# A layernorm inside a local transformer: statistics by token rows on VectorE, applied by GpSimd, in place of sums by matmul

## The chip, the cores and the metric

The kernel runs on one core of a Trainium2 chip. A core has five engines that run their own instruction streams and meet at semaphores: TensorE (PE; its weight loads are listed apart as PEld), VectorE (DVE), ScalarE (ACT), GpSimd (POOL) and SyncE (SP), which here only issues DMA transfers. The metric is the device time of one execution in microseconds. The kernel before takes 4091.11 us, the median of three runs between 4088.63 and 4092.11.

## The reference

Two transformer blocks with adaptive layernorm over 16 sequences of 256 tokens by 128 channels, all in fp32. The first block has a linear attention, and in the place of its feed-forward part a whole local transformer of six layers. That inner transformer is where the change lies:

```python
for i in range(DEPTH):                       # 6 layers
    x = attn_layer(shift_tokens(x), ...) + x # 16 heads of 64, windows of 32 tokens
    x = ffn_layer(shift_tokens(x), ...) + x

def ffn_layer(x, g, bln, W1, b1, W2, b2):
    mu = x.mean(-1, keepdims=True)
    var = ((x - mu) ** 2).mean(-1, keepdims=True)
    xn = (x - mu) / jnp.sqrt(var + 1e-05) * g + bln
    hg = xn @ W1 + b1
    a, gate = jnp.split(hg, 2, -1)
    return a * jax.nn.gelu(gate, approximate=False) @ W2 + b2
```

The mean and the variance go over the 128 channels of a token. The local attention normalises each q and k head, rotates it, takes scores over the own window and the one before, a softmax, and a weighted sum. The second block is an attention with relative position bias and a plain feed-forward part.

## The kernel before

The work is cut into 8 units of two sequences, 512 tokens each. Activations are held with the channels on the partitions and the tokens along the free axis: a tile is 128x512. The state of the inner transformer stays in SBUF for all six layers, one tile `zs[u]` for each unit, with a margin of 32 columns for the window before and one column for the shift of tokens.

The kernel has three stages: the first block's attention (to about 265 us), the local transformer (to about 3525 us) and the second block. The local transformer is one software pipeline written as a loop over `n` (L1065). A turn of the loop starts one pair of head groups (two of the eight pairs of heads) of one unit, so a unit takes four turns, a layer 32, and the six layers 192; the work that belongs to earlier turns is done in the same turn, with lags of 1 to 10. Around the change, a turn does this in order:

- GpSimd scales two k by their inverse norms (`scaled`, L802); these come from DRAM by the transfer kn.
- TensorE merges the weighted values into the output (`merging`, L942); after the unit's fourth merge the attention's result is added to the state (L955).
- In odd turns TensorE turns the inverse norms rk upright (`norms_rows`, L781), VectorE copies them (L783), and SyncE stores them (rkh, L785), from where kn is read (`widened`, L793).
- GpSimd rotates q and k of the turn before (`rotate`, four instructions at L721), using `got`, a copy of VectorE's `sent` with swapped partitions that SyncE makes by DMA (L715, L716).
- TensorE flips the probabilities (L906, copied by VectorE at L911); GpSimd divides the next ones (L898).
- In even turns the sums of squares (L729), copied by ScalarE (L738); then the weighted sums (L921), copied out by ScalarE (L936) and VectorE (L934); then the scores (L858), on VectorE their maxima (L870, L872).
- In even turns `norms_inverse`: TensorE turns the sums (L747), VectorE makes a first guess (L749, L758), and GpSimd does three Newton steps (L765 to L773), which end in rk (L772) and rq.
- The next two projections of q and k (L705): ScalarE squares them (L708) between the exponentials (L880), and VectorE writes `sent` (L710) and r (L713) for each.

The feed-forward part of a unit is a generator, `ffn(u, i)`. Its pieces are put into the turns by `go_on(behind)`, which is called four times in a turn: after the flips (L1098), after the weighted sums (L1111), after `norms_inverse` (L1127), and after the first of the two projection pairs (L1134). A `yield` ends a piece. The first piece of a unit comes at L1127 in the turn of its last merge, the second at L1134 of that turn, the third at L1098 of the next; four yields are one turn. So the pieces are: the mean (L968) and its subtraction (L970); the square (L973); the variance, the power and a copy of the inverse deviations over 128 columns (L977, L985, L987, L989); one turn later the turning of these and the scaling (L994, L995, L996); then at one turn's distance the gates (L1004, L1006), the other half (L1014, L1018) and the last matmul with the addition to the state (L1027, L957). Units follow one another every four turns, so each period of four turns has one call's first piece and the later pieces of the call before.

The order on TensorE, VectorE, ScalarE and GpSimd is the order in which the program is written (`manual_schedule`, L130 to L135 and L1062). SyncE's queue is not in that list, and the trace shows its transfers in another order than that of the program.

Matmul results go through four PSUM banks that are handed round (`bank()`, L58, with `psum(es, 4, 3)` at L601): the fifth allocation waits until the first is read out. In a feed-forward tile pool with one buffer each lie `fx` and `fs`, which this function uses.

Of the kernel before, what the change touches and what calls it, by code (L numbers as in the profile page):

```python
# [14 lines left out]
ALU = mybir.AluOpType  # L15
# [29 lines left out]
def adaln_kernel(  # L45
# [12 lines left out]
    def bank():  # L58
        return stage["ps"].tile([128, 512], F32, tag="mm", name="mm")

    def two(ap):
        return ap.rearrange("p (s t) -> p s t", s=2)
# [537 lines left out]
    with ExitStack() as es:  # L600
# [362 lines left out]
        def ffn(u, i):  # L963


            src = zs[u][:, :, PAD : PAD + L]
            pm = bank()
            nc.tensor.matmul(pm, mean128, src, start=True, stop=True)  # L968
            xn = ftile("fx")
            nc.vector.tensor_tensor(two(xn), src, two(pm), ALU.subtract)  # L970
            yield
            sq = ftile("fs")
            nc.scalar.activation(sq, xn, AF.Square)  # L973
            yield
            pv = bank()
            for t in range(4):
                nc.tensor.matmul(  # L977
                    pv[:, t : t + 1],
                    sq[:, t * 128 : (t + 1) * 128],
                    mean128[:, 0:1],  # L980
                    start=True,
                    stop=True,
                )
            ve = small("ve", (128, 4))
            nc.vector.tensor_scalar(ve, pv[:, 0:4], 1e-5, None, ALU.add)  # L985
            rs = small("rs", (128, 4))
            nc.gpsimd.tensor_tensor(rs, ve, half[:, 0:4], ALU.pow)  # L987
            ex = ftile("fs", (128, 4, 128))
            nc.gpsimd.tensor_copy(ex, rs.unsqueeze(2).to_broadcast([128, 4, 128]))  # L989
            for _ in range(4):  # L990
                yield
            rb = bank()
            for t in range(4):
                nc.tensor.transpose(rb[:, t * 128 : (t + 1) * 128], ex[:, t], ident)  # L994
            nc.vector.tensor_tensor(xn, xn, rb, ALU.mult)  # L995
            nc.vector.tensor_scalar(xn, xn, bcol(i, "g"), bcol(i, "b"), ALU.mult, ALU.add)  # L996
            for _ in range(4):
                yield
            w1, w2 = wffs[i]
            gates = []  # L1000
            for c, n in enumerate(FFC):
                pg = bank()
                c0 = FFH + c * 128
                nc.tensor.matmul(pg[0:n, :], w1[:, c0 : c0 + n], xn, start=True, stop=True)  # L1004
                gt = ftile("fg", bufs=3)
                nc.scalar.activation(gt[0:n, :], pg[0:n, :], AF.Gelu, bias=bcol(i, f"g{c}", n))  # L1006
# [14 lines left out]
            yield  # L1021
            yield
            yield
            yield
            py = bank()
            for c, n in enumerate(FFC):
                nc.tensor.matmul(  # L1027
                    py, w2[0:n, c, :], gates[c][0:n, :], start=(c == 0), stop=(c == 2)
                )
            add_to_state(u, py, bcol(i, "b2"))  # L1030
# [589 lines left out]
```

## Time and profile before

| | |
|---|---|
| median of three runs | 4091.11 us (4088.63 to 4092.11) |
| profiled execution, span from first to last instruction | 4089.6 us |
| local transformer, of this | about 265 to 3525 us |
| TensorE's granted clock, mean | 0.980; 1.00 between 1000 and 3440 us |
| time from one unit's mean (L968, L970) to the next unit's | 63.5 to 70 us |

The page gives no other time of the profiled execution than its span; what lies around it can only be read from the runs, whose median is 1.5 us above.

In the views below a line of the chain of waits has a start, a length and then engine, tile and line of the code; it follows the work that ended last back through what released it. A line of a timeline has start, length, engine, line, operation, output and inputs with their shapes, and how many were put together; in brackets stands the time for which the engine was idle before, with what ended it. "mm" is any of the four rotating PSUM banks, "fx" and "fs" the tiles of the feed-forward part, "rs" the inverse deviations, "z" the state. TensorE is listed with two passes for a matmul in fp32, so a matmul counts as two instructions; a turning (transpose) counts as one.

### The profile page before, as it was taken

How to read it: one execution, taken by the hardware profiler on the slowest of the kernel's cores; microseconds unless marked ns; L12 is line 12 of the kernel's file. 1: busy time of each engine (PE TensorE's matmuls, PEld its weight loads, DVE VectorE, ACT ScalarE, POOL GpSimd, SP SyncE). 2: the span in 40 equal slices, each digit the busy share in tenths (PEclk: the TensorE clock that was granted, in tenths of full speed). 3: DMA queues.
4: the chain of work that ended last, by engine and by line, in shares of the span. 5: the costliest groups of instructions: out<-in, count | busy, mean ns of one | idle time of the engine just before them, and what ended most of it. 6: DMA issues, size and time to landing. Idle time of an engine off the chain costs nothing.

```text
span 4089.6 us, 117058 instructions
## 1 busy us (share of the span) xinstructions
PE 3824.8 (94%) x44534; PEld 2533.5 (62%) x44534; DVE 2944.4 (72%) x6006; ACT 2797.5 (68%) x9683; POOL 2653.6 (65%) x3374
## 2 busy tenths in 40 slices
PE   7877899999999999999999999999999999799998
PEld 4534666666666666666666666666666666455554
DVE  6756777777777777777777777777777775476664
ACT  4536777777777777677777777776777776366665
POOL 6437777767776777677776777777777665255453
PEclk9878999999999999999999999999999999899999
DMA  1334454445545445454554444454545443200000
GB/s 42 42 83 118 121 126 115 123 118 128 126 124 127 117 122 125 117 127 113 128 131 121 121 123 116 123 130 120 127 107 131 115 118 79 63 1 6 9 6 9
DMA packets 316617, 408.82 MB, mean 100 GB/s; under 512 B 48745, under 2 KB 212632, under 8 KB 316056
## 3 DMA queue, kind: packets, MB, share of 16 engines
q1 hardware_dynamic: 316056, 401.33, 39.6%
q8 instruction: 353, 5.78, 0.6%
q14 instruction: 208, 1.70, 0.1%
HBM read 178.26 MB, written 21.56 MB: 49 GB/s over the span
## 4 chain that ended last, share of the span: by engine, by line
PE 53%; DVE 16%; ACT 16%; issue 6%; POOL 5%; DMA 2%; SPq 1%; ACTq 0%; DVEq 0%; POOLq 0%
PE mm L921 8%; ACT pr L880 7%; PE y L942 6%; PE mm L705 6%; PE sim L858 6%; DVE sent L710 3%; PE mm L729 3%; PE mm L1027 3%; ACT sq L708 2%; PE mm L1014 2%; PE mm L1398 2%; DVE mx L870 2%; PE mm L906 2%; PE sim L1325 2%; DVE k L713 2%
## 5 line engine op out<-in xcount | busy, mean ns | idle before, releaser
L880 ACT ACTIVATE pr<-sim,nb,rq 128x64 f32<-128x64 f32 x3072 | 1229.2, 453 | 366.9 <-DVE nb L872 307.5
L880 ACT ACTIVATION_READ_ACCUMULATOR pr<-sim,nb,rq 128x1 f32 x3072 | 783.1, 255 | 0.0
L942 PEld LDWEIGHTS y<-zx,wvo 128*128 128x128 f32 x6144 | 715.8, 192 | 93.0 <-issue 88.3
L802 POOL TENSOR_TENSOR k<-k,kn 128x512 f32<-128x512 f32 x384 | 483.7, 1274 | 435.9 <-DMA kn<-rkh 434.4
L705 PE MATMUL mm<-z,wqk 128*128 128x512 f32 x1536 | 710.3, 604 | 13.4 <-DMA wqk<-in_L_ffn_Wqkv_dram 7.9
L942 PE MATMUL y<-zx,wvo 128*128 128x128 f32 x6144 | 717.9, 275 | 2.2 <-ACT zx L936 1.8
L721 POOL TENSOR_TENSOR q<-q,got 128x512 f32<-128x512 f32 x384 | 488.5, 1272 | 300.4 <-DMA got<-sent 173.2
L710 DVE SCALAR_TENSOR_TENSOR sent<-mm,vec,rope 128x512 f32<-128x512 f32 x768 | 571.0, 743 | 117.4 <-ACT sq L708 109.9
L934 DVE COPY zx<-mm 128x512 f32<-128x512 f32 x384 | 255.3, 674 | 375.0 <-PE mm L921 374.5
L708 ACT ACTIVATE sq<-mm 128x512 f32<-128x512 f32 x768 | 475.6, 619 | 30.9 <-PE mm L705 29.5
L721 POOL TENSOR_TENSOR k<-k,got 128x512 f32<-128x512 f32 x384 | 496.4, 1293 | 0.0
L705 PEld LDWEIGHTS mm<-z,wqk 128*128 128x128 f32 x1536 | 281.9, 192 | 328.5 <-issue 252.5
L921 PE MATMUL mm<-prT,xw 64*128 64x256 f32 x3072 | 452.5, 401 | 11.6 <-ACT n L738 6.4
L921 PEld LDWEIGHTS mm<-prT,xw 64*128 64x128 f32 x3072 | 326.7, 188 | 179.9 <-DVE rsum L893 38.6
L898 POOL TENSOR_TENSOR pr<-pr,rsum 128x512 f32<-128x512 f32 x384 | 392.3, 1043 | 14.0 <-PE mm L1004 7.4
L936 ACT COPY zx<-mm 128x512 f32<-128x512 f32 x384 | 227.0, 596 | 248.9 <-PE mm L921 248.4
L870 DVE TENSOR_REDUCE mx<-sim 128x8 f32<-128x512 f32 x384 | 263.1, 685 | 138.7 <-PE sim L858 137.9
L1368 POOL TENSOR_TENSOR pr<-pr,rsum 128x256 f32<-128x256 f32 (+1 forms) x256 | 205.1, 832 | 242.2 <-DVE rsum L1366 218.2
L858 PEld LDWEIGHTS sim<-k,q 64*32 64x32 f32 x24576 | 264.3, 106 | 80.9 <-issue 56.4
L858 PE MATMUL sim<-k,q 64*32 64x64 f32 x24576 | 299.5, 227 | 11.8 <-POOL k L802 6.5
L1354 ACT ACTIVATE pr<-lg,nm 128x128 f32<-128x128 f32 (+1 forms) x512 | 226.3, 443 | 117.3 <-DVE nm L1343 109.4
L713 DVE SCALAR_TENSOR_TENSOR q<-mm,vec,rope 128x512 f32<-128x512 f32 x384 | 284.5, 741 | 0.0
(253 smaller groups left out, 6244.7 us busy)
## 6 DMA issues: line engine op xcount, KB each, us to landing
got<-sent SPq DMA_DIRECT2D x1536, 128.0 KB
kn<-rkh SPq DMA_DIRECT2D x768, 128.0 KB
xw<-rows SPq DMA_DIRECT2D x384, 128.0 KB
rows<-xt SPq DMA_DIRECT2D x96, 128.0 KB
wqk<-in_L_ffn_Wqkv_dram SPq DMA_DIRECT2D x48, 128.0 KB
bhome<-brow SPq DMA_DIRECT2D x1, 3072.0 KB
wv<-in_L_ffn_Wqkv_dram SPq DMA_DIRECT2D x12, 256.0 KB
wo<-in_L_ffn_Wo_dram SPq DMA_DIRECT2D x12, 256.0 KB
```

Source lines behind the costliest of these rows:

```text
L705: nc.tensor.matmul(pp, wqk[:, j, :], xs, start=True, stop=True)
L708: nc.scalar.activation(sq, pp, AF.Square)
L710: nc.vector.scalar_tensor_tensor(two(sent[:, j, :]), two(pp), scale, tab[1], ALU.mult, ALU.mult)
L713: nc.vector.scalar_tensor_tensor(r, two(pp), scale, tab[0], ALU.mult, ALU.mult)
L721: nc.gpsimd.tensor_tensor(r, r, two(got[:, j, :]), ALU.add)
L802: nc.gpsimd.tensor_tensor(k, k, two(kn), ALU.mult)
L858: nc.tensor.matmul(sims[par][32 * c : 32 * c + 32, c0 : c0 + 64], q[r, s, t0 : t0 + 32], k[r, s, t0 : t0 + 64], start=False, stop=True, sk ...
L870: nc.vector.tensor_reduce(mx, sim.rearrange("p (b k) -> p b k", b=8), AX.X, ALU.max)
L880: nc.scalar.activation(pr[:, x, st, par, :], sims[par][:, b * 64 : (b + 1) * 64], AF.Exp, bias=nbs[par][:, b : b + 1], scale=rn[:, par, b ...
L898: nc.gpsimd.tensor_tensor(prf, prf, rsum[:, x].unsqueeze(2).to_broadcast([128, 8, 64]), ALU.mult)
L921: nc.tensor.matmul(pz[par][:, w * 256 : (w + 1) * 256], xw[r, (2 * k + w) % 8, :], prT[r, :, 64 * k + 32 * w : 64 * k + 32 * w + 32], star ...
L942: nc.tensor.matmul(py[:, j * 128 : (j + 1) * 128], vo[:, h, :], zx[:, h % 2, h // 2, :], start=(h == 0), stop=(h == 2 * NP - 1), skip_grou ...
```

## The change

The layernorm of `ffn` is computed with the tokens on the partitions. TensorE turns the state (four turnings of 128x128), ScalarE copies the result to SBUF (`fs`), VectorE makes mean and variance of each token by `bn_stats` and `bn_aggr`, four instructions each, and adds the epsilon. GpSimd takes the power -0.5 and applies both in four instructions of 128x128, with mean and inverse deviation as columns. TensorE turns the four blocks back as it did before with the copied deviations, and VectorE scales with g and adds b, reading PSUM. The mean by matmul, its subtraction, the square, the variance by matmul, the copy of the deviations over 128 columns and the multiplication by them are gone. The number of yields is the same; the statistics stand in the second piece, where the square was.

```diff
-            src = zs[u][:, :, PAD : PAD + L]
-            pm = bank()
-            nc.tensor.matmul(pm, mean128, src, start=True, stop=True)
-            xn = ftile("fx")
-            nc.vector.tensor_tensor(two(xn), src, two(pm), ALU.subtract)
-            yield
-            sq = ftile("fs")
-            nc.scalar.activation(sq, xn, AF.Square)
-            yield
-            pv = bank()
-            for t in range(4):
-                nc.tensor.matmul(
-                    pv[:, t : t + 1],
-                    sq[:, t * 128 : (t + 1) * 128],
-                    mean128[:, 0:1],
-                    start=True,
-                    stop=True,
-                )
+            pt = bank()
+            for t in range(4):
+                s, c = t // 2, PAD + 128 * (t % 2)
+                nc.tensor.transpose(
+                    pt[:, t * 128 : (t + 1) * 128], zs[u][:, s, c : c + 128], ident
+                )
+            xt = ftile("fs", (128, 4, 128))
+            nc.scalar.copy(xt.rearrange("p t d -> p (t d)"), pt)
+            yield
+            stats = small("bst", (128, 4, 6), 2)
+            mv = small("bmv", (128, 4, 2), 2)
+            for t in range(4):
+                nc.vector.bn_stats(stats[:, t, :], xt[:, t, :])
+            for t in range(4):
+                nc.vector.bn_aggr(mv[:, t, :], stats[:, t, :])
             ve = small("ve", (128, 4))
-            nc.vector.tensor_scalar(ve, pv[:, 0:4], 1e-5, None, ALU.add)
+            nc.vector.tensor_scalar(ve, mv[:, :, 1], 1e-5, None, ALU.add)
+            yield
             rs = small("rs", (128, 4))
             nc.gpsimd.tensor_tensor(rs, ve, half[:, 0:4], ALU.pow)
-            ex = ftile("fs", (128, 4, 128))
-            nc.gpsimd.tensor_copy(ex, rs.unsqueeze(2).to_broadcast([128, 4, 128]))
+            for t in range(4):
+                nc.gpsimd.tensor_scalar(
+                    xt[:, t, :],
+                    xt[:, t, :],
+                    mv[:, t, 0:1],
+                    rs[:, t : t + 1],
+                    ALU.subtract,
+                    ALU.mult,
+                )
             for _ in range(4):
                 yield
             rb = bank()
             for t in range(4):
-                nc.tensor.transpose(rb[:, t * 128 : (t + 1) * 128], ex[:, t], ident)
-            nc.vector.tensor_tensor(xn, xn, rb, ALU.mult)
-            nc.vector.tensor_scalar(xn, xn, bcol(i, "g"), bcol(i, "b"), ALU.mult, ALU.add)
+                nc.tensor.transpose(rb[:, t * 128 : (t + 1) * 128], xt[:, t], ident)
+            xn = ftile("fx")
+            nc.vector.tensor_scalar(xn, rb, bcol(i, "g"), bcol(i, "b"), ALU.mult, ALU.add)
```

More of the change, by code (lines that the diff above doesn't have):

```diff
@@ L963, in ffn @@
         def ffn(u, i):
-            src = zs[u][:, :, PAD : PAD + L]
-            pm = bank()
-            nc.tensor.matmul(pm, mean128, src, start=True, stop=True)
-            xn = ftile("fx")
-            nc.vector.tensor_tensor(two(xn), src, two(pm), ALU.subtract)
-            yield
-            sq = ftile("fs")
-            nc.scalar.activation(sq, xn, AF.Square)
-            yield
-            pv = bank()
-            for t in range(4):
-                nc.tensor.matmul(
-                    pv[:, t : t + 1],
-                    sq[:, t * 128 : (t + 1) * 128],
-                    mean128[:, 0:1],
-                    start=True,
-                    stop=True,
-                )
-            ve = small("ve", (128, 4))
-            nc.vector.tensor_scalar(ve, pv[:, 0:4], 1e-5, None, ALU.add)
+            pt = bank()
[6 more added lines that the diff above has]
+            nc.scalar.copy(xt.rearrange("p t d -> p (t d)"), pt)
+            yield
+            stats = small("bst", (128, 4, 6), 2)
[4 more added lines that the diff above has]
+                nc.vector.bn_aggr(mv[:, t, :], stats[:, t, :])
+            ve = small("ve", (128, 4))
+            nc.vector.tensor_scalar(ve, mv[:, :, 1], 1e-5, None, ALU.add)
+            yield
             rs = small("rs", (128, 4))
             nc.gpsimd.tensor_tensor(rs, ve, half[:, 0:4], ALU.pow)
-            ex = ftile("fs", (128, 4, 128))
-            nc.gpsimd.tensor_copy(ex, rs.unsqueeze(2).to_broadcast([128, 4, 128]))
+            for t in range(4):
[7 more added lines that the diff above has]
+                )
             for _ in range(4):
```

## The prediction

> **What bounds the kernel now.** I read the page first, then the chain of waits, then the timelines of one feed-forward period engine by engine. The page says that no engine but TensorE is near full, and that half of the chain is not TensorE:
>
> ```profile
> PE 3824.8 (94%) x44534; PEld 2533.5 (62%) x44534; DVE 2944.4 (72%) x6006; ACT 2797.5 (68%) x9683; POOL 2653.6 (65%) x3374
> ...
> PE 53%; DVE 16%; ACT 16%; issue 6%; POOL 5%; DMA 2%; SPq 1%; ACTq 0%; DVEq 0%; POOLq 0%
> ```
>
> The changed function runs 48 times (6 layers by 8 units), once every four turns of the main loop, some 66.2 us apart. In each period I call the four turns T0 (the statistics' first step, L968, stands there), T1 (L977), T2 (L994) and T3. The chain of waits, in the period that starts T0 at 2301, with start and length in us:
>
> ```profile
> 2301.84 1.06 PE mm L968 x2
> 2302.90 3.43 PE mm L705 x8
> 2306.33 3.57 PE y L942 x32
> 2309.90 0.87 PE mm L906 x8
> 2310.77 2.58 PE mm L1027 x6
> 2313.35 0.79 PE mm L977 x8
> ...
> 2327.42 0.26 POOL rk L772
> ...
> 2328.01 0.88 PE mm L906 x8
> 2328.89 0.44 PE mm L994 x4
> ```
>
> TensorE carries T0 and T1, so removing L968 and L977 looks like a clear gain. But T2 begins with the turning of rk (L781), and rk comes from GpSimd, whose program in T1 is: scale two k, four rotations (L721), the power and the copy of this function (L987, L989), two divisions (L898), then the Newton steps that end in rk. In the timelines of GpSimd and TensorE (start, length, idle time before in brackets):
>
> ```profile
> 2311.45 1.27 POOL L802 TENSOR_TENSOR k<-k,kn 128x512 f32<-128x512 f32 x1 [8.88 <-DMA kn<-rkh]
> 2313.25 1.27 POOL L802 TENSOR_TENSOR k<-k,kn 128x512 f32<-128x512 f32 x1 [0.53 <-DMA kn<-rkh]
> ...
> 2319.41 1.02 POOL L987 TENSOR_TENSOR rs<-ve,half 128x4 f32<-128x4 f32 x1
> 2320.49 0.61 POOL L989 COPY fs<-rs 128x512 f32<-128x512 f32 x1
> 2321.06 2.04 POOL L898 TENSOR_TENSOR pr<-pr,rsum 128x512 f32<-128x512 f32 x2
> ```
>
> ```profile
> 2327.73 0.28 PE L781 MATMUL mm<-ident,rk 128*32 128x128 f32 x1 [0.72 <-POOL rk L772]
> ```
>
> I went through the timelines of 44 of the 48 periods for this one point. They fall in three classes. *Late* (17): as above, GpSimd runs without a pause from the second scaling to rk, and TensorE waits for it, 0.79 us on average. *Spare* (16): GpSimd pauses 1.52 us on average before the Newton steps, waiting for VectorE's L758, and rk is ready 0.67 us before TensorE asks. *Short* (11): it pauses 0.38 us and rk is ready 0.14 us ahead. So rk sets TensorE's pace in nearly every period, or would after a small gain. The late class comes from SyncE's queue, where kn stands behind transfers that must wait for this turn's VectorE:
>
> ```profile
> 2296.26 0.66 SPq L785 DMA_DIRECT2D rkh<-rkT  x1
> 2306.56 0.53 SPq L715 DMA_DIRECT2D got<-sent  x1
> 2307.14 0.58 SPq L716 DMA_DIRECT2D got<-sent  x1
> 2307.77 2.51 SPq L793 DMA_DIRECT2D kn<-rkh  x4
> ```
>
> In other periods kn follows rkh 2 us later. The order in that queue isn't the program's.
>
> **The change part by part.** TensorE: out go L968 (1.05 us on the chain) and L977 (0.79); in come four turnings of the state, which cost 0.44 like L994; the turning back stays. That is 1.40 us less in a period, 67 us over 48. On the chain, asked stretch by stretch, L968 stands 37 times and L977 42 times, so at most 37 x 0.61 + 42 x 0.79 = 56 us if nothing else holds TensorE.
>
> ScalarE: a square of 0.64 us leaves T0 between the exponentials; a copy out of PSUM (0.59 as L936, 0.70 as L813) comes ahead of them. The first exponential starts 1.0 to 1.1 us after the scores, when the first maxima and their scaling are done; turnings and copy need about as long. I take zero; without that cover it would be 0.5 us a period.
>
> VectorE in T2: L995 (0.67) and L996 (mean 1.11, from 0.55 to 1.63) become one scaling out of PSUM, 0.69 as L1313. That is 1.1 us less work. In the late class VectorE and TensorE reach the maxima within 0.1 us of each other, elsewhere VectorE waits for the scores; so at most 0.1 us shows. I take zero.
>
> L996 runs from SBUF to SBUF, and its spread goes with GpSimd's activity (0.55 in the tail of the stage, where GpSimd is idle); L1313, out of PSUM, stays between 0.659 and 0.693. The Trainium skill's "SBUF — State Buffer", section "Who interferes with whom", has the rule: a VectorE instruction with at most one SBUF input outside the two-port modes does not contend with GpSimd. By it the new scaling is free of the lock, which agrees with the row and adds nothing to the sum.
>
> VectorE in T0: L970 (0.65 from start to start) leaves the front of the projections; four statistics over 128 columns, four small merges and ve come between the two pairs of them. No row shows the statistics. One of them lies between 0.20 (a 128x64 scaling takes 0.21) and 0.38 (128x128 scalings of L326); the slope from L985 (4 columns, 0.16) to L870 (512 columns, 0.69) gives 0.29. A merge is a small instruction, 0.09 to 0.16. The sum is 1.3 to 2.3 us; I take 1.6, nearest the slope. Behind it wait the second pair's sent and so its got. In periods where VectorE is ahead, the pair starts 3.0 us after the first now, of which some 0.3 are a wait for ScalarE, so 1.2 us are added; where VectorE is behind, 1.6 - 0.65 = 1.0. I take g = 1.1 us (0.5 to 1.5). L1027 needs a PSUM bank that this pair releases: it comes out level with TensorE's earlier arrival, nothing added.
>
> GpSimd in T1: the copy (0.57 start to start) goes, four scalings of 128x128 with two column operands come. L1270 does 128x256 with two column operands in 0.555, L767 128x64 with constants in 0.243; the line between them gives 0.35 each, less 0.01 of overlap. 4 x 0.34 - 0.57 = 0.79 us more, which I call p. Bounds: 4 x 0.24 - 0.57 = 0.4 and 4 x 0.55 - 0.57 = 1.6. Queued behind are the divisions, the Newton steps, rk, L781, and with it all of T2; the next scaling (L802) too, but it ends 1 us ahead of the scores that read it. The power now waits for a ve made a turn earlier; it never waited in mid-kernel.
>
> The Trainium skill's "GPSIMD Engine Reference", section "4.1 Engine selection", tells the author to leave elementwise work to VectorE, yet calls one-input work on GpSimd roughly line rate. By line rate (section 3.1: 128 lanes, 1.03 cycles an element at 1.2 GHz) a scaling would take 0.11 us and the four 0.44, cheaper than the copy, an estimate from that page; the late class would then cost nothing. L1270's 0.555 us for 256 columns contradicts it, and the row decides.
>
> Sum at L781. Late: rk comes p later; the second got is hidden there (its rotation starts 7.2 us or more after its sent, against 4.4 where GpSimd waits for the transfer), and TensorE's saving only lengthens its wait: 17 x 0.79 = +13.4 us. Spare: rk moves by p + g - 1.52 = 0.37, and TensorE may come 0.67 earlier: 16 x (0.37 - 0.67) = -4.8. Short: their got already lands 5.5 to 6.2 us after its sent, so I count half of g: 0.79 + 0.5 - 0.38 - 0.14 = 0.77, by 11 = +8.5. Together +17.1. The last call runs alone: from L968 at 3502.8 to L1004 at 3512.1 it takes 9.3 us; new 0.6 + 0.7 + 1.6 + 1.0 + 1.4 + 0.7 + 0.7 and 0.3 of hand-overs, 7.0, so -2.3. Sum +14.8 us. The profiled execution's span is 4089.6, the runs' median 4091.1, 1.5 above it; 4091.1 + 14.8 gives 4106.
>
> **The rivals.** *The gate opens (faster).* If SyncE's queue lets kn pass ahead of got in every period, the late class vanishes: its 17 periods lose the 0.79 wait and behave as spare ones. 17 x -1.09 - 4.8 + 8.5 - 2.3 = -17, so 4074; with p and g at zero too, TensorE's whole 56 us come through: 4033. It decides from the point where rk is ready before TensorE's new arrival. For it speaks that 27 of 44 periods have that order today; against, that nothing in the change is aimed at it.
>
> *The gate closes everywhere.* The opposite order: first got ahead of kn in the 27 other periods too. They would pay 0.79 of wait and p: 27 x 1.58 + 13.4 - 2.3 = +54, so 4145. For it speaks that L970 no longer delays the first pair of sent, so got is ready sooner.
>
> *All of it hidden.* With p = 0.4 and g = 0.5, late costs 6.8, spare gives 10.7, short costs 1: -5 with the last call, 4086 to 4091. Against it stands L1270's row.
>
> **How the numbers follow.** The forecast has 0.45, the open gate 0.25, the closed one 0.15, all hidden 0.15. A difference under 0.2% (8 us) can't be told from none. Of the forecast 0.36 lie above +8 us, 0.07 within and 0.02 below; the open gate gives 0.24 faster and 0.01 same, the closed 0.15 slower, the hidden case 0.03 faster, 0.10 same, 0.02 slower. Faster 0.29, same 0.18, slower 0.53. The forecast's own range is 4085 to 4130. The full one goes down to 4050, between the open gate's two values, and up to 4145.
>
> **What would show it.** Right: TensorE's busy time falls by some 60 us while its wait for rk at L781 grows from 49 us in the middle of the kernel to over 80; four scalings near 0.35 us each on GpSimd; the third rotation waiting longer for got. Wrong: L781 without idle time and rk ready early (the gate opened), statistics far from 0.3 us, or exponentials in T0 that wait for the new copy. A different share of periods with got ahead of kn would also overturn the sum.

## The result, and the profile after

The changed kernel takes 4214.3 us (median of four runs, 4209.5 to 4239.9) against 4089.9 for the kernel before on the same chip: a ratio of 1.032, with a 95% interval of 1.029 to 1.035. It is slower, the side that the prediction held likeliest (0.53), but by 124 us where 15 were forecast, and 69 us above the upper end of the range.

The busy times and the shares of the chain in the page of the changed kernel, whose profiled execution has a span of 4211.1 us:

```profile
PE 3806.6 (90%) x44246; PEld 2517.4 (60%) x44246; DVE 2917.2 (69%) x6294; ACT 2797.8 (66%) x9683; POOL 2764.3 (66%) x3518
...
PE 38%; ACT 17%; DVE 17%; POOL 15%; issue 7%; SPq 3%; DMA 3%; POOLq 0%; ACTq 0%; DVEq 0%
```

TensorE's share of the chain has fallen from 53% to 38%, and GpSimd's has risen from 5% to 15%, although GpSimd is still busy for only 66% of the span. An engine that is idle a third of the time now sets the pace, because its work of T1 stands in one block ahead of rk. The chain of waits, in the period that corresponds to the one shown of before:

```profile
2325.54 1.00 POOL rs L985
...
2326.63 3.16 POOL fs L987 x4
2329.80 2.01 POOL pr L898 x2
...
2335.96 0.26 POOL rk L772
...
2336.27 0.28 PE mm L781
2336.55 0.89 PE mm L906 x8
```

The four scalings (L987) take 3.16 us and all of it is on the chain: power, scalings, divisions, Newton steps, rk, its turning (L781), and behind that all of T2. The groups of instructions that are new (busy time in all and mean ns of one behind the first bar):

```profile
L987 POOL TENSOR_SCALAR fs<-fs,bmv,rs 128x128 f32<-128x128 f32 x192 | 150.4, 795 | 5.2
L978 DVE BATCH_NORM_STATS2 bst<-fs 128x6 f32<-128x128 f32 x192 | 41.4, 278 | 0.5 <-ACT fs L973 0.5
L1001 DVE TENSOR_SCALAR fx<-mm,vec 128x512 f32<-128x512 f32 x48 | 38.7, 807 | 11.4 <-PE mm L999 11.1
L980 DVE BATCH_NORM_AGGREGATE bmv<-bst 128x2 f32<-128x6 f32 x192 | 17.3, 152 | 0.0
```

A scaling on GpSimd takes 0.795 us where the prediction had 0.35. The statistics, of which no row of before told anything, came out as estimated (0.278 us, taken 0.29). TensorE's matmul for the turning of rk, of before and of after; behind the last bar stands the idle time ahead of it, in us:

```profile
L781 PE MATMUL mm<-ident,rk 128*32 128x128 f32 x96 | 27.4, 286 | 48.4 <-POOL rk L772 48.1
```

```profile
L781 PE MATMUL mm<-ident,rk 128*32 128x128 f32 x96 | 29.9, 311 | 185.2 <-POOL rk L772 184.9
```

The table has the averages of the same few points over the first 45 of the 48 periods of every kernel, always counted from the first TensorE instruction of T0 of the changed function. All experiments can be read from it. "Third rotation" is its start, "pause" GpSimd's idle time before the Newton steps, "rk" the end of L772, "idle" TensorE's wait ahead of L781 in T2.

| kernel | ratio to before (95%) | period | third rotation | pause | rk | idle |
|---|---|---|---|---|---|---|
| before | 1 | 66.08 | 14.20 | 0.63 | 25.45 | 0.37 |
| after | 1.032 (1.029 to 1.035) | 69.09 | 14.66 | 0.00 | 27.81 | 3.40 |
| e1, (mult, add), two small operations more | 1.0213 (1.0195 to 1.0232) | 68.21 | 14.72 | 0.01 | 27.09 | 2.62 |
| e2, no scalings | 0.9894 (0.9880 to 0.9909) | 65.23 | 14.58 | 0.28 | 24.80 | 0.60 |
| e3, before + GpSimd work | 1.0247 (1.0228 to 1.0265) | 68.30 | 14.36 | 0.01 | 27.58 | 2.23 |
| e4, statistics in T1 | 1.0222 (1.0207 to 1.0237) | 68.18 | 13.90 | 0.00 | 27.06 | 2.93 |
| e5, scalings on ScalarE | 0.9907 (0.9880 to 0.9934) | 65.36 | 15.12 | 0.62 | 24.69 | 0.49 |
| e6, scalings on VectorE | 1.0095 (1.0077 to 1.0113) | 67.04 | 15.02 | 1.19 | 25.88 | 0.00 |
| e7, (add, mult) | 1.0115 (1.0098 to 1.0131) | 67.22 | 14.72 | 0.00 | 26.48 | 2.10 |
| e8, e5 with statistics in T1 | 0.9895 (0.9880 to 0.9909) | 65.23 | 14.58 | 0.71 | 24.31 | 0.28 |
| e9, before + VectorE work | 1.0003 (0.9995 to 1.0012) | 66.12 | 14.65 | 0.36 | 25.67 | 0.42 |
| e10, e4 and e7 together | 1.0051 (1.0034 to 1.0067) | 66.84 | 13.95 | 0.13 | 25.89 | 1.74 |
| e11, after + filler on TensorE | 1.0299 (1.0285 to 1.0313) | 68.95 | 14.94 | 0.00 | 28.09 | 1.60 |

Between before and after, the period grew by 3.01 us and the idle time by 3.03. rk comes 2.36 us later and TensorE is ready for it 0.94 us earlier (its own saving); with the 0.28 us by which rk used to be ready ahead, used up but for 0.01, that makes the 3.03. By this sum TensorE's saving was made, and waited away at the same place. Cut at the start of rk's turning, 2.09 of the 3.01 us lie ahead of it and 0.92 behind it, in T2 and T3.

### The profile page after: what moved, and what is told of

The parts are those of the page before. It is cut to its first block, busy times and chain, and to the rows that moved or that the text cites. A ratio compares the mean times of both kernels' runs of the same rounds, so it can differ in the third digit from the quotient of the medians.

```text
span 4211.1 us, 116958 instructions
## 1 busy us (share of the span) xinstructions
PE 3806.6 (90%) x44246; PEld 2517.4 (60%) x44246; DVE 2917.2 (69%) x6294; ACT 2797.8 (66%) x9683; POOL 2764.3 (66%) x3518
## 3 DMA queue, kind: packets, MB, share of 16 engines
q14 instruction: 213, 1.74, 0.1%
## 4 chain that ended last, share of the span: by engine, by line
PE 38%; ACT 17%; DVE 17%; POOL 15%; issue 7%; SPq 3%; DMA 3%; POOLq 0%; ACTq 0%; DVEq 0%
ACT pr L880 8%; PE mm L921 8%; PE sim L858 5%; DVE sent L710 4%; POOL fs L987 3%; DMA got<-sent 3%; ACT sq L708 2%; POOL pr L898 2%; DVE q L713 2%; PE mm L705 2%; PE mm L1019 2%; PE mm L1403 2%; PE sim L1330 2%; PE mm L906 2%; DVE k L713 2%
## 5 line engine op out<-in xcount | busy, mean ns | idle before, releaser
L880 ACT ACTIVATE pr<-sim,nb,rq 128x64 f32<-128x64 f32 x3072 | 1231.7, 456 | 247.5 <-DVE nb L872 176.1
L880 ACT ACTIVATION_READ_ACCUMULATOR pr<-sim,nb,rq 128x1 f32 x3072 | 791.8, 258 | 0.0
L705 PE MATMUL mm<-z,wqk 128*128 128x512 f32 x1536 | 705.0, 601 | 14.2 <-DMA wqk<-in_L_ffn_Wqkv_dram 7.8
L936 ACT COPY zx<-mm 128x512 f32<-128x512 f32 x384 | 225.1, 587 | 438.0 <-PE mm L921 438.0
L921 PE MATMUL mm<-prT,xw 64*128 64x256 f32 x3072 | 465.8, 416 | 8.5 <-ACT n L738 2.5
L705 PEld LDWEIGHTS mm<-z,wqk 128*128 128x128 f32 x1536 | 279.3, 192 | 301.8 <-issue 237.4
L921 PEld LDWEIGHTS mm<-prT,xw 64*128 64x128 f32 x3072 | 335.3, 200 | 187.7 <-DVE prT L911 38.6
```

Of the source, the lines that this page charges most:

```text
L705: nc.tensor.matmul(pp, wqk[:, j, :], xs, start=True, stop=True)
L880: nc.scalar.activation(pr[:, x, st, par, :], sims[par][:, b * 64 : (b + 1) * 64], AF.Exp, bias=nbs[par][:, b : b + 1], scale=rn[:, par, b ...
L921: nc.tensor.matmul(pz[par][:, w * 256 : (w + 1) * 256], xw[r, (2 * k + w) % 8, :], prT[r, :, 64 * k + 32 * w : 64 * k + 32 * w + 32], star ...
```

## The experiments

Theory from here on: GpSimd's time between T1's first instruction and rk is the gate, and the scalings are dearer than I had priced them. Rivals: VectorE's statistics in T0, which send the second pair of transfers later; and TensorE's clock, which may fall in the longer waits.

### e0: what a scaling costs on GpSimd

The kernel before with seven groups of four GpSimd scalings on unused tiles at its end (the kinds differ in operations, operands and width):

```diff
+        for _ in range(4):
+            nc.gpsimd.tensor_scalar(fb[:, 0:128], fa[:, 0:128], c0, c1, ALU.subtract, ALU.mult)
...
+        for _ in range(4):
+            nc.gpsimd.tensor_scalar(fb[:, 0:128], fa[:, 0:128], c0, c1, ALU.mult, ALU.add)
```

> The kernel before, with 28 GpSimd scalings on scratch tiles added behind its last turn, four of each of seven kinds: 128x128 (subtract, mult) with two column operands, the same at 128x256, then 128x128 as (mult, add) and as (add, mult) with columns, (subtract) with one column, (subtract, mult) and (mult, add) with constants. The changed kernel's scalings took 0.79 us each where 0.35 was forecast from rows with (mult, add). If the kind of operation sets the price, (mult, add) takes 0.30 to 0.40 us and (subtract, mult) 0.79; if the column operands set it, both column kinds take 0.79 and the constant kinds 0.35; if it is contention in the loop, all take 0.30 to 0.45 here.

The groups, in order: (subtract, mult) with two columns; the same over 256 columns of data; (mult, add) and (add, mult) with two columns; subtract alone with one column; (subtract, mult) and (mult, add) with constants:

```profile
L1514 POOL TENSOR_SCALAR bias<-bias,vec 128x128 f32<-128x128 f32 x4 | 3.2, 799 | 0.3
...
L1516 POOL TENSOR_SCALAR bias<-bias,vec 128x256 f32<-128x256 f32 x4 | 4.9, 1222 | 0.4
...
L1518 POOL TENSOR_SCALAR bias<-bias,vec 128x128 f32<-128x128 f32 x4 | 1.8, 454 | 0.4
...
L1520 POOL TENSOR_SCALAR bias<-bias,vec 128x128 f32<-128x128 f32 x4 | 1.8, 451 | 0.4
...
L1522 POOL TENSOR_SCALAR bias<-bias,vec 128x128 f32<-128x128 f32 x4 | 2.4, 606 | 0.4
...
L1524 POOL TENSOR_SCALAR bias<-bias 128x128 f32<-128x128 f32 x4 | 2.6, 645 | 0.3
...
L1526 POOL TENSOR_SCALAR bias<-bias 128x128 f32<-128x128 f32 x4 | 1.2, 301 | 0.3
```

The kind of operation decides, and the operands add to it. The changed kernel's 0.795 us appear here as 0.799, where VectorE does nothing at all, so contention isn't what makes them long. With two columns, (subtract, mult) costs 0.80 where (mult, add) and (add, mult) cost 0.45; with constants 0.645 against 0.301. So the kind is worth 0.34 us, and two column operands 0.15. The kinds differ per element: from 128 to 256 columns (subtract, mult) grows by 0.42 us, while (mult, add) grows by 0.10 (0.454 here, 0.555 for L1270 of the kernel before, which is of that kind). One row of the kernel before could have warned me. L431 adds one constant, a kind that is neither of the two cheap pairs, and takes nearly three times as long as L1270 for twice the columns (group of before):

```profile
L431 POOL TENSOR_SCALAR fq<-fq 128x512 f32<-128x512 f32 x8 | 12.1, 1517 | 0.7 <-ACT fq L420 0.2
```

### e1 and e7: the same normalisation in the cheaper kind

Both replace `(x - mean) * rs`. e1 computes `x * rs + nm` with `nm = -mean * rs` made by two small GpSimd operations of 0.20 and 0.23 us; e7 computes `(x + nm) * rs` with `nm = -mean` made by VectorE in T0, so GpSimd has no operation more. e7:

```diff
+            nm = small("nm", (128, 4))
+            nc.vector.tensor_scalar(nm, mv[:, :, 0], -1.0, None, ALU.mult)
...
-                    mv[:, t, 0:1],
+                    nm[:, t : t + 1],
...
-                    ALU.subtract,
+                    ALU.add,
```

> The changed kernel with the scaling written as x * rs + (-mean * rs): (mult, add) in place of (subtract, mult), and two small GpSimd instructions of 128x4 more for the second column. Theory gate (GpSimd's time between the rotations and rk sets the period): if a (mult, add) takes 0.35 us, GpSimd has 3.16 - 1.4 - 0.5 = 1.3 us less in every period, 48 x 1.3 = 60 us: 4150. If it takes 0.79 as well, 0.5 more: 4235. Theory statistics (VectorE's late got is what costs): 4210, whatever the scaling takes.

> The changed kernel with the same normalisation in another kind of scaling: (add, mult) with the mean negated by one small VectorE operation in T0, so GpSimd has no operation more. Gate theory (GpSimd's time between T1's first operation and rk sets the turn, about 1 us per us): scalings 0.45 instead of 0.79 each, 48 x 4 x 0.34 = 65 us off the changed kernel, about 4148, ratio to before about 1.015, mean idle before rk's turn about 2.2 us per turn instead of 3.4. Statistics theory (VectorE's T0 work sends the key transfers late, and that is what costs): no gain or a loss, since VectorE has one operation more in T0, 4205 to 4225.

e1 takes 4174.3 us (ratio 1.0213), e7 4132.9 (1.0115). In e1 the scalings take 0.448 us each; less the two small operations that is 0.94 us a period, 45 us in all, and 1.032 - 1.0213 is 44 us. In e7 another kind of operation in four instructions a period, and one small VectorE operation for it, are worth 2% of the kernel's time: 1.032 - 1.0115 is 84 us, for 48 x 4 x 0.34 = 65 us of GpSimd work. The gate theory stands, the statistics theory is wrong for e7, which has one VectorE operation more in T0. The 19 us beyond 65 are taken up under e11.

### e2: no scalings at all

The scalings are left out and the copy is multiplied by 0.01 instead, so x isn't normalised; statistics, power and turnings stay.

```diff
-            nc.scalar.copy(xt.rearrange("p t d -> p (t d)"), pt)
+            nc.scalar.activation(xt.rearrange("p t d -> p (t d)"), pt, AF.Identity, scale=0.01)
...
-            for t in range(4):
-                nc.gpsimd.tensor_scalar(
...
```

> The changed kernel without the four GpSimd scalings; mean and deviation are computed and not applied, and ScalarE's copy multiplies by 0.01 to keep the values bounded. GpSimd does 3.2 us less in a period than the changed kernel and 0.6 less than before. Theory gate: rk comes early, TensorE's saving shows, 4030 to 4070. Theory statistics: got stays late, 4150 or more.

4042.1 us, ratio 0.9894: 172 us below the changed kernel for 48 x 3.16 = 152 us of GpSimd's work. The idle time at L781 falls from 3.40 to 0.60 us, and TensorE's saving appears in the time.

### e3: the kernel before with the change's GpSimd load

Three (subtract, mult) scalings on an unused tile behind the copy (2.4 us), nothing else:

```diff
+            for t in range(3):
+                nc.gpsimd.tensor_scalar(
+                    scr[:, 0:128], scr[:, 128:256], ve[:, 0:1], rs[:, 0:1], ALU.subtract, ALU.mult
+                )
```

> The kernel before, with three GpSimd scalings (subtract, mult) of 128x128 on a scratch tile behind the copy of the deviations: some 2.4 us more of GpSimd in T1 and nothing else. Theory gate: late periods pay 2.4, spare ones 2.4 - 1.52 - 0.67 = 0.2, short ones 2.4 - 0.52 = 1.9: 17 x 2.4 + 16 x 0.2 + 11 x 1.9 = 65 us, 4155, or more if the delay makes later transfers late too. Theory statistics: 4090.

4186.3 us, ratio 1.0247, +103 us, with the statistics by matmul as before. The turning of rk on TensorE (its line and rk's are one further down here):

```profile
L782 PE MATMUL mm<-ident,rk 128*32 128x128 f32 x96 | 28.8, 300 | 130.9 <-POOL rk L773 127.5 <-DVE k L714 3.1
```

48 x 2.4 = 115 us were added and 103 came out, where I had expected 65. The pause of 0.63 us and the lead of rk of 0.28 us, which the kernel before has on the average, are both used up, so by the gate alone some 71 us should have come out (2.4 - 0.91, times 48). The other 32 are not explained by this run. Two things go with them: got stands ahead of kn in 22 of 45 periods instead of 18, and in 18 periods instead of 2 the clock was low behind the wait (see e11). Together with e2 this shows the cause from both sides: the same kind of load takes 172 us away when it is removed from the changed kernel, and adds 103 to the kernel before.

### e4 and e9: the statistics' part, with and without the long block

e4 is the changed kernel with the statistics one piece later, on VectorE in T1, so that they no longer stand between the two pairs of sent:

```diff
             yield
+            yield
             stats = small("bst", (128, 4, 6), 2)
...
-            yield
             rs = small("rs", (128, 4))
...
-            for g in list(parts):
+            for g in reversed(list(parts)):
```

The last two lines are in `go_on`: the newer call's piece goes ahead of the older call's.

> The changed kernel with the statistics (bn_stats, bn_aggr, +1e-5) one piece later, on VectorE in T1 ahead of the older call's piece instead of in T0. The sent tiles of T0 then end about 1 us earlier (8.1 us into the turn instead of 9.0). Late-transfer theory: the third rotation's wait for its transfer falls by about 1 us in the 18 periods where a transfer stands ahead of kn, some 0.5 to 1 us in the others, 20 to 45 us off, about 4170 to 4195. Gate theory with GpSimd's work alone: pow now has to wait for the statistics only if they end after the second rotation of T1; GpSimd's sum is unchanged, so within 10 us of the changed kernel, 4205 to 4225.

e9 is the kernel before with 1.0 us of VectorE work at that place of T0 (four bn_stats whose result isn't used, and one small operation):

```diff
+            for t in range(4):
+                nc.vector.bn_stats(spare[:, t, :], xn[:, t * 128 : (t + 1) * 128])
+            nc.vector.tensor_scalar(spare[:, :, 0], spare[:, :, 1], 1e-5, None, ALU.add)
```

> The kernel before with 1.0 us more of VectorE work in T0, behind the first piece's square: four bn_stats on the tile that it has and one small operation, whose results nothing reads. It moves the end of T0's last sent tile from 8.1 to about 9.1 us, as the change does, and leaves GpSimd's work as it is. This measures the term g alone. By the gate the 18 periods that idle already (0.92 us) pay up to 1 us each, the others have 0.45 us of slack and 1.06 us of pause in front of Newton's steps: 10 to 20 us slower, ratio 1.002 to 1.005. If late transfers cost by themselves in every period: 48 x 1.0 = 48 us, ratio 1.012. If they cost only with GpSimd's long sum: ratio 0.999 to 1.001.

The change had moved the end of T0's last sent from 8.08 to 9.04 us into the period. e4 moves it back to 7.64 and gains 38 us (4176.5, ratio 1.0222): the third rotation starts 0.76 us earlier and rk comes 0.75 us earlier, all of it. The gain lies in the 27 periods with kn ahead of got (68.54 to 66.96 us); the 18 others stay as they are (69.91 and 70.00). e9 moves it from 8.08 to 8.91, and nothing happens (4089.3, ratio 1.0003). The third rotation starts 0.45 us later there too, but the pause falls from 0.63 to 0.36 and rk's lead from 0.28 to 0.13, and the period is the same within 0.04 us. The turning of rk in e9, to be held against the 48.1 us of before:

```profile
L782 PE MATMUL mm<-ident,rk 128*32 128x128 f32 x96 | 27.5, 287 | 54.9 <-POOL rk L773 51.6 <-DVE sent L711 2.5
```

So the late transfers cost nothing by themselves, and some 38 us once GpSimd has no pause left. I had expected 10 to 20 us of e9 by the gate; the slack in front of and behind the Newton steps held more than I had counted.

### e10: both remedies

e4 and e7 together; the parts are those shown above, with the negated mean made in T1.

> The changed kernel with both partial remedies, (add, mult) scalings with a negated mean and the statistics in T1. If the loss has the two causes and they add: 1.032 - (1.032 - 1.0115) - (1.032 - 1.0222) = 1.0017, some 4090 to 4100, about as before. If the two overlap (either one relieves the same wait of the third rotation): 1.007 to 1.0115, 4115 to 4133. If the second remedy moves pow behind the late statistics and so costs by itself once GpSimd is shorter: above 1.0115.

4109.0 us, ratio 1.0051 (1.0034 to 1.0067): between adding (1.0017) and overlapping (1.007 to 1.0115). Alone, e4 takes 9.8 thousandths off the changed kernel's ratio and e7 20.5, 30.3 together; both at once take 26.9. So most of the two adds. What is left against before is a block on GpSimd that is still some 1.2 us longer (4 x 0.45 - 0.57).

### e5 and e6: the scalings on another engine

Both move the power behind T1's two scalings of k (`early` is a list that the loop empties there) and take the four scalings off GpSimd. e5 gives them to ScalarE with a column scale and bias, in T1, one piece later than GpSimd had them:

```diff
-            nc.gpsimd.tensor_tensor(rs, ve, half[:, 0:4], ALU.pow)
+            early.append(
+                lambda: nc.gpsimd.tensor_tensor(rs, ve, half[:, 0:4], ALU.pow)
+            )
...
+            nc.vector.scalar_tensor_tensor(nm, mv[:, :, 0], -1.0, rs, ALU.mult, ALU.mult)
...
-                nc.gpsimd.tensor_scalar(
+                nc.scalar.activation(
...
+                    AF.Identity,
+                    bias=nm[:, t : t + 1],
+                    scale=rs[:, t : t + 1],
```

> The changed kernel with the four scalings on ScalarE in T1 (column scale and bias), one small VectorE operation for the bias, and pow moved ahead on GpSimd, right behind T1's two scalings of the state. GpSimd has less in T1 than the kernel before (no copy of 0.57, pow no longer at the end). Gate theory: idle before rk's turn below that of the kernel before (under 0.4 us per turn) if ScalarE takes the 4 operations (about 0.25 each by the smallest activation rows, an estimate) without delaying T2's exponentials; 4020 to 4070, ratio 0.983 to 0.996. Rival: ScalarE or VectorE in T1 is the next gate and the turn grows by the scalings' 1 us: 4080 to 4130.

e6 gives them to VectorE as (subtract, mult), ahead of the older call's piece in T1:

```diff
-                nc.gpsimd.tensor_scalar(
+                nc.vector.tensor_scalar(
...
-            for g in list(parts):
+            for g in reversed(list(parts)):
```

> The changed kernel with the four scalings on VectorE in T1, ahead of the older call's piece, and pow moved ahead on GpSimd right behind T1's two scalings of the state. Gate theory: GpSimd is relieved of 3.16 us per turn against the changed kernel and 0.57 against before; 4020 to 4070, as with the scalings on ScalarE. Rival: the four operations on VectorE (some 0.25 to 0.35 each, an estimate from 0.28 for a statistics row of the same tile) stand ahead of the older call's piece and of T2's rkT, so the turn grows by their 1.0 to 1.4 us: 4080 to 4130.

e5 takes 4046.7 us, ratio 0.9907: faster than the kernel before. ScalarE's four scalings take 0.483 us each, twice my estimate, and wait for little but the small VectorE operation nm (its group; the last part is the idle time in front):

```profile
L992 ACT ACTIVATE fs<-fs,nm,rs 128x128 f32<-128x128 f32 x192 | 79.2, 483 | 36.6 <-DVE nm L990 35.0 <-DVE zx L934 1.6
```

ScalarE had the room: in the changed kernel it idles 438 us in all ahead of the copies of the weighted sums (L936), which TensorE makes late, and 246 in e5. In e5's page TensorE's busy time is down by 54 us, close to the 60 that the prediction had for the change, and half of the chain is TensorE again:

```profile
PE 3771.2 (93%) x44246; PEld 2484.3 (61%) x44246; DVE 2954.9 (73%) x6342; ACT 2873.8 (71%) x9875; POOL 2617.1 (65%) x3326
...
PE 49%; ACT 19%; DVE 16%; POOL 6%; issue 5%; SPq 3%; DMA 2%; ACTq 0%; POOLq 0%; DVEq 0%
```

e6 takes 4124.0 us, ratio 1.0095. The rival's time came out, for a reason that I had not named. The scalings' durations on VectorE (least, median, most in ns), and then the timelines of VectorE and GpSimd in a period of e6 where got stands ahead of kn:

```profile
L989 DVE TENSOR_SCALAR fs<-fs,bmv,rs x192: 332/1166/1321, 457.9 to 3541.4; 128x128 f32<-128x128 f32 x192
```

```profile
2333.27 3.76 DVE L989 TENSOR_SCALAR fs<-fs,bmv,rs 128x128 f32<-128x128 f32 x3
```

```profile
2333.22 1.26 POOL L721 TENSOR_TENSOR k<-k,got 128x512 f32<-128x512 f32 x1
2334.45 1.28 POOL L721 TENSOR_TENSOR q<-q,got 128x512 f32<-128x512 f32 x1
2335.68 1.26 POOL L721 TENSOR_TENSOR k<-k,got 128x512 f32<-128x512 f32 x1
```

A scaling that takes 0.33 us by itself takes 1.25 here: three of them end in step with three rotations. In the 18 periods of this order the period is 69.04 us, in the other 27 it is 65.71. The Trainium skill's "SBUF — State Buffer", section "Who interferes with whom", says that a VectorE instruction in a two-port mode, which a scaling from SBUF to SBUF can enter, and a GpSimd instruction exclude each other for their whole length. The rows agree: each VectorE scaling lasts about as long as one rotation.

### e8: e5 with the statistics in T1

The statistics move as in e4, and the power goes between the second and third rotation:

```diff
-                for m in (2 * (n - 1), 2 * (n - 1) + 1):
-                    rotate(m, qs[m], got.pop(m))
+                rotate(2 * n - 2, qs[2 * n - 2], got.pop(2 * n - 2))
...
+            while early:
+                early.pop()()
+            if 0 <= n - 1 < N:
+                rotate(2 * n - 1, qs[2 * n - 1], got.pop(2 * n - 1))
```

> The kernel with the scalings on ScalarE, with the statistics in T1 instead of T0, and pow between T1's second and third rotation, where GpSimd waits for a transfer (15.1 - 14.0 = 1.1 us a turn on the average before the third rotation). Theory of two causes (GpSimd's sum in T1, and the late transfers that VectorE's statistics in T0 make): in the 18 periods in which the turn of rk still idles 1.21 us, the transfers come 1 us earlier, 18 x 1.0 = 18 us, so 4020 to 4035, ratio 0.983 to 0.988, better than the 0.9907 of the scalings on ScalarE alone. Rival (the transfers' lateness counts only together with GpSimd's long sum, or VectorE's work in T1 is as dear): 4040 to 4060.

4046.9 us, ratio 0.9895 (0.9880 to 0.9909): not to be told from e5. The rival's time came out. The idle time at L781 fell from 0.49 to 0.28 us a period, which is 9 us at most. In the 27 periods with kn ahead of got the third rotation starts 0.95 us earlier and wins nothing, since TensorE doesn't wait there (0.01 us in e5). In the 18 others it starts no earlier (16.29 and 16.38 us), so the 18 us that I had hoped for could not come.

### e11: is it the clock?

In the changed kernel, a period with a long wait at L781 looks like this on TensorE (timeline, with the idle time in brackets), and below are stretches of it with the busy times of the five engines, and then the granted clock (0.52 and 0.51), the DMA share and GB/s:

```profile
816.64 0.40 PE L781 MATMUL mm<-ident,rk 128*32 128x128 f32 x1 [4.24 <-POOL rk L772]
816.83 1.91 PE L906 MATMUL mm<-ident,pr 128*128 128x128 f32 x8
818.53 1.06 PE L999 MATMUL mm<-ident,fs 128*128 128x128 f32 x4
```

```profile
816.50:818.00 1.50, 1.36 (x7) 1.37 (x8) 0.35 (x2) 0.00 (x0) 1.50 (x4) 0.52 0.02 5
818.00:820.00 2.00, 2.00 (x10) 1.67 (x10) 1.67 (x3) 0.00 (x0) 2.00 (x3) 0.51 0.07 16
820.00:822.00 2.00, 2.00 (x51) 1.52 (x50) 1.49 (x4) 0.83 (x2) 2.00 (x3) 1.00 0.00 0
```

After 4.24 us of idle time the clock is at half for some 3.5 us, and the eight flips take 1.91 us; they take 1.04 and the four turnings 0.60 in the same place of the kernel before. In 31 of 45 periods of the changed kernel the granted clock was low (under 0.95 on the mean) in the 3.5 us from the turning of rk on, and flips or turnings back ran slow; in the kernel before it was 2. Over all runs, the shortest wait with this behind it was 1.93 us (e1) and the longest without 3.58 (e1 too). The Trainium skill's "TensorE: Matmul & The Clock Gate", section "Why this matters for your kernels", warns of idle gaps over about 3 us for this; the rows agree on the mechanism, and show that here it can begin at less than 2.

e11 fills the wait with 20 turnings of the identity that serve nothing (2.2 us), in T2 only:

```diff
+            for _ in range(fill):
+                nc.tensor.transpose(pt[:, 128:256], ident, ident)
...
-                home = norms_rows(rk)
+                home = norms_rows(rk, 20 if n % 4 == 3 and n >= 14 else 0)
```

> The changed kernel with 20 turnings of the identity (0.11 us each from start to start, 2.2 us together) on TensorE right ahead of the turning of rk in T2, into an unused part of the same bank: work that serves nothing, put where TensorE idles 3.4 us on the average. GpSimd, and so the time at which rk comes, is as in the changed kernel. Clock theory: the long idle lets the granted clock fall to about 0.5 (the eight flips behind it take 1.91 instead of 1.04 us in such turns, 30 of 45 turns against 2 before, some 1.2 us each, 35 us in all); with the idle time cut to about 1.2 us most of these vanish: 25 to 35 us less, less about 5 us where the idle time was shorter than the filler, so 4180 to 4195, ratio 1.023 to 1.027, and the busy time of the flips (L906) falls from 228 to about 210 us. If the clock plays no part in the time: 4210 to 4225, ratio 1.030 to 1.033.

4207.5 us, ratio 1.0299 (1.0285 to 1.0313), which can't be told from the changed kernel's 1.032. The clock came back in large part. The groups of the flips and of the turnings back, first in the changed kernel, then in e11 (where their lines are two further down):

```profile
L906 PE MATMUL mm<-ident,pr 128*128 128x128 f32 x1536 | 228.2, 295 | 7.2 <-DVE q L713 5.9 <-DVE k L713 1.2
...
L999 PE MATMUL mm<-ident,fs 128*128 128x128 f32 x192 | 43.4, 367 | 2.9 <-POOL fs L987 2.9
```

```profile
L908 PE MATMUL mm<-ident,pr 128*128 128x128 f32 x1536 | 214.2, 283 | 5.3 <-DVE q L713 4.4 <-DVE k L713 0.7
...
L1001 PE MATMUL mm<-ident,fs 128*128 128x128 f32 x192 | 35.0, 310 | 2.9 <-POOL fs L989 2.9
```

These 22 us of TensorE's busy time did not come out as time. From rk's turning to the next T0 it is 40.31 us before, 41.23 in the changed kernel and 40.72 with the filler, so 0.51 us a period were gained behind the gate, 23 us over 45 periods. But rk's turning starts 0.37 us later in this run. Part of that is the order in SyncE's queue: got stood ahead of kn in 24 periods instead of 18, and such periods are 0.9 us longer (69.37 against 68.48 in e11). So the slow clock follows from the wait and takes time of its own behind the gate, but this run doesn't show it in the kernel's time, and its 7 us of gain are within its uncertainty. The 23 us are not the whole of it either: in e11 the clock was still low in 14 periods.

The kept traces allow another comparison. Not every wait brings the clock down, so take, from all runs, the periods with a wait of 2.0 to 3.6 us, and the time from rk's turning to the next T0:

| order | clock low | full clock |
|---|---|---|
| got ahead of kn | 40.99 us (59 periods, mean wait 2.98) | 39.83 us (18 periods, 2.73) |
| kn ahead of got | 41.45 us (31 periods, 2.70) | 40.00 us (16 periods, 2.69) |

A low clock goes with 1.2 to 1.5 us more behind the gate. In the changed kernel the next turning of rk then comes some 0.3 us earlier than otherwise, which gives a part back. For 29 low periods more than before this leaves some 25 to 35 us of the 124, an estimate from a comparison of periods and not from an experiment. It also fits e7: of the 1.87 us a period that e7 gains on the changed kernel, 1.32 lie ahead of rk's turning and 0.55 behind it, 25 us in all, and its clock was low in 20 periods instead of 31. That this is where the 19 us come from is argued, not shown.

## The prediction, point by point

**The gate.** Right. L781's wait for rk was named as what sets the period, with GpSimd's block in T1 as its cause, and the changed kernel, e1, e2, e3, e5 and e7 all move with that block.

**p, GpSimd's four scalings.** This is the step that failed: "the line between them gives 0.35 each" and p = +0.79, with bounds of 0.4 and 1.6. A scaling takes 0.795 us. From the start of the power to the start of the divisions it is 2329.77 - 2325.49 = 4.28 us after and 2321.06 - 2319.41 = 1.65 before, so p = +2.6. Two things went wrong. The line was drawn between L767, which takes constants, and L1270, which takes columns; a 128-column (mult, add) with columns takes 0.45, not 0.35. And both rows were of the kind (mult, add), while the change subtracts first; that is the other 0.34. The upper bound, four times L1270's 0.55, took it that half the width can't cost more, which holds only within one kind. L431 was overlooked: with nearly three times L1270's time for twice the width it shows that the kind matters. It would have widened the bounds, but not given the size: scaled to 128 columns it makes 0.38 us, an estimate, about half of what was measured.

The estimate by line rate from the Trainium skill's "GPSIMD Engine Reference", section 3.1, 0.11 us a scaling, is four times below the cheapest kind with columns (0.45) and seven times below the one used.

**The sum with p as measured.** The prediction's own formulas with p = 2.6 give: late 17 x 2.6 = 44; spare 16 x (2.6 + 1.1 - 1.52 - 0.67) = 24; short 11 x (2.6 + 0.5 - 0.38 - 0.14) = 28; the last call -1.0 as it came out (8.3 us from L969 to L1009 instead of 9.3, forecast -2.3). That is +95 us of the 124. The other 29 or so are not in the formulas. They lie in the periods with got ahead of kn, the late class: there rk came 2.40 us later (26.08 to 28.48), but the period grew by 3.94 (65.98 to 69.92); in the others rk came 2.33 later and the period grew by 2.39. 18 x 1.54 is 28 us. These are the periods with the longest waits (4.54 us), where the clock falls. By the estimate under e11 the clock, at some 25 to 35 us, is about as large; no term of the prediction stood for it, and that it is this part is argued, not shown.

**g, the late transfers.** The size was right (0.96 us measured against 1.1 taken), and so were the statistics: from the first statistic to the next sent 1.38 us in the period at 2315, at the lower end of "1.3 to 2.3". That the late class hides it was right as well: there the third rotation did not start later (15.45 and 15.34). GpSimd's wait for got ahead of the rotations grew in all from 173 to 262 us, as forecast. What it is worth depends on the rest, and e9 and e4 show both ends: nothing while GpSimd pauses, some 38 us when it doesn't.

**TensorE.** "Busy time falls by some 60 us" came out as 18 in the changed kernel, and as 54 in e5 and 51 in e8. Flips and turnings back make up most of the difference: 228.2 + 43.4 us in the changed kernel, 206.7 + 29.9 in e8. The matmul's wait for rk grew from 48 to 185 us in the whole kernel; the forecast had it growing to over 80. The "49 us in the middle of the kernel" that it started from is the whole kernel's figure: between 1000 and 3440 us the wait is 15.6 us before and 115.9 after.

**ScalarE and VectorE in T2 at nothing.** ScalarE's wait for VectorE's nb ahead of the exponentials (L880) fell from 307.5 to 176.1 us; that for the projections (L705) rose from 43.9 to 68.0. The scaling out of PSUM (L1001) took 0.81 us, not the 0.69 of L1313, which reads no columns; in the period shown it ends 2.6 us before the maxima start, and cost nothing that shows.

**The rivals.** Neither order of SyncE's queue came about: got stands ahead of kn in 18 of 45 periods before and after. The state that "the gate closes everywhere" describes did come, TensorE waiting in all 45 periods, by GpSimd's length rather than by the queue, which is why 4145 was too low as well. "All of it hidden" fell with p.

## What to carry to other kernels

Before pricing an operation by a row of the same engine and shape, see that the row is of the same kind, operands included: on GpSimd here (subtract, mult) in place of (add, mult) made a scaling 1.8 times as long, and with the mean negated elsewhere the kernel was 84 us faster. Slack on a path is one reserve for all that lands on it: e9's delay was free where the pause was there, and a delay of that size cost some 38 us (e4) behind a block that had used it up. When an edit that saves time on the full engine makes the kernel slower, look for the engine that feeds it late and move that work to one that waits there anyway: with the scalings on ScalarE (e5, e8) the same layernorm is about 1% faster than the kernel before, where on GpSimd it is 3% slower.

## What the runs showed of the hardware

- GpSimd: a 128x128 scaling takes 0.30 us as (mult, add) with constants, 0.45 with two columns, 0.80 as (subtract, mult) with two columns; the last grows by 0.42 us for 128 further columns, (mult, add) by 0.10.
- VectorE: bn_stats over 128 columns takes 0.278 us (four in a row 0.86), bn_aggr 0.152 (four in a row 0.36). A 128x128 scaling from SBUF to SBUF takes 0.33 us alone and 1.25 beside GpSimd's rotations.
- TensorE: a wait of 4.24 us brought the granted clock to 0.52 for 3.5 us. Waits from 1.93 us on could do it, and one of 3.58 did not.
